# The last routed group taken apart: layernorm and logits in two pieces, one more shared expert at the end, a third set of weight buffers

## The chip, the cores and the metric

The kernel runs on one core of one Trainium2 chip. The metric is the device time of one launch in microseconds (us); of several runs the median is taken. In the profile's rows PE is TensorE's matmuls, PEld its weight loads, DVE VectorE, ACT ScalarE, POOL GpSimd, SP the engine that queues most DMAs.

## The reference, cut to what matters

There are 64 batches of 128 tokens with 128 features, each with 77 context rows of 96 features.

```python
x = x + xattn(layernorm(x), ctx_768)       # 16 heads of 64, softmax over 77 keys
x = x + ffn(layernorm(x))

def ffn(x2):                               # x2: 8192 tokens of 128
    logits = x2 @ router_w.T               # 8 experts
    _, idx = top_k(softmax(logits), 2)
    gate = scatter(logits at idx)
    for e in range(8):                     # inner width 176
        moe += gate[:, e] * ((silu(x2 @ w1[e].T) * (x2 @ w3[e].T)) @ w2[e].T)
    return moe + shared expert of the same shape, for all tokens
```

The first line is the attention with its residual, the second the mixture of experts: each token goes to two of eight experts and to a shared one.

## The kernel before

**Attention.** The 64 batches form 16 groups of four (`G = 4`, `T = 512` tokens). A unit is one batch and eight of its heads; there are 128 units, and each is worked on in two steps, so that group g occupies the steps 16g to 16g + 15 of a written plan (`at(step, ...)`). In one pass of the loop, TensorE computes the scores of the unit two ahead (`scores`, tile ps), the product with the values of a finished batch (`out`, tile py), and the transposed weights (tile pa). VectorE takes maxima and sums (tiles mx, sc, sm), ScalarE the exponentials, GpSimd the normalization (tile at).

**Routing.** When a group's batches are done, a `Router` takes it over: `stats` (layernorm statistics on VectorE, and one power on GpSimd, tile rs_f), `normed` (ScalarE scales the rows into the tile pay), `transpose` (TensorE, tile pxT_f, copied by ScalarE into x2T), `logits` (TensorE, tile pl), `choose` and `choose_second` (sixteen small VectorE operations that find two experts), `place` (the rank of each token among those of its expert; matmuls into pr, then VectorE up to the tile row), and `send`: eight indirect DMAs from GpSimd that scatter the rows to DRAM (tensor sent). The shared expert follows (`shared_up`, `shared_rest`, `shared_down`), and x1 is put away in DRAM (`park`).

**Experts.** The groups form three sets (`SETS = (9, 5, 2)`). After a set's last group, `tables` works out which 128-row block belongs to which expert. Four blocks make a `Quad`; the sets have 20, 12 and 6 of them. A quad loads its rows (xb, SP), copies its four experts' weights within SBUF (`weights`, tile w: two copies on ScalarE, two on VectorE), transposes (pt), multiplies (`first`: p; `rest`: ph; `down`: pq), and scatters its result (tile y) with four indirect DMAs from GpSimd (`answer`, tensor answers). A `Combine` per group loads x1 and the two answers of each token (tile ya), adds them on VectorE and stores them.

**Order.** All engines run what is written in the order in which the plan emits it; the order of each engine's instructions is fixed when the program is built. Quads of a set are spread evenly over the steps of the next set's groups. The last seven quads of the second set (`KEPT = 7`), the shared expert of the last group and the six quads of the last set run behind the attention, in `ending()`, as 14 jobs in a row; what is written in `ahead_of[k]` is emitted ahead of job k. There the last group, number 15, is routed: statistics ahead of job 0, transpose and logits ahead of 1, choice ahead of 2, ranks ahead of 3, sends ahead of 4, tables ahead of 5.

In the text "quad 1.7" is quad 7 of the second set (the sets are numbered 0, 1, 2). Only buffers that matter here: the tile y has two, pay one, w eight, vo (values) four, ya three.

Of the kernel before, what the change touches and what calls it, by code (L numbers as in the profile page):

```python
# [8 lines left out]
F32 = mybir.dt.float32  # L9
# [26 lines left out]

KEPT = 7

# [22 lines left out]
def xattn_moe_kernel(  # L61
# [32 lines left out]
    def weights_of(engine, w, q, n, name):  # L94

        to = ffn.tile([128, WALL], F32, tag="w", name=f"{name}_{q}", bufs=2 * QUAD)
        to = to[:, : 4 * n].rearrange("p (m d) -> p m d", d=n)
        engine.dma_start(out=to, in_=w[:, 4 * q : 4 * (q + 1), :])
        return to
# [161 lines left out]
    class Norm:  # L261
# [4 lines left out]

        def stats(self):
            st = small.tile([128, G, 6], F32, tag="st", name=f"st_{self.name}")
            self.mv = small.tile([128, G, 2], F32, tag="mv", name=f"mv_{self.name}")
            for b in range(G):  # L270
                nc.vector.bn_stats(st[:, b, :], self.src[:, b, :])
            for b in range(G):
                nc.vector.bn_aggr(self.mv[:, b, :], st[:, b, :])
            ve = small.tile([128, G], F32, tag="ve", name=f"ve_{self.name}")
            nc.vector.tensor_scalar(ve, self.mv[:, :, 1], EPS, None, ALU.add)
            self.rs = small.tile([128, G], F32, tag="rs", name=f"rs_{self.name}")
            nc.gpsimd.tensor_tensor(self.rs, ve, mhalf, ALU.pow)

        def scale(self, to):

            self.to = to
            shift = small.tile([128, G], F32, tag="shift", name=f"shift_{self.name}")
            nc.vector.scalar_tensor_tensor(shift, self.mv[:, :, 0], -1.0, self.rs, ALU.mult, ALU.mult)
            for b in range(G):
                nc.scalar.activation(
                    to[:, b, :],
                    self.src[:, b, :],
                    AF.Identity,
                    scale=self.rs[:, b : b + 1],
                    bias=shift[:, b : b + 1],  # L290
                )

        def transposed(self, tag):
            pt = bank(f"pxT_{self.name}")
            for b in range(G):
                nc.tensor.transpose(pt[:, b * 128 : (b + 1) * 128], self.to[:, b, :], ident)
            xT = grp.tile([D, T], F32, tag=tag, name=f"{tag}_{self.name}")
            nc.scalar.copy(xT, pt)
            return xT

# [4 lines left out]
    class Attention:  # L305
# [75 lines left out]
        def values(self, p, i):  # L381

            bs = (2 * p, 2 * p + 1)
            if i == 0:
                for b in bs:
                    self.vo[b] = bat.tile([128, NT, D], F32, tag="vo", name=f"vo_{self.g}_{b}", bufs=4)
                    k = KS * (self.g % 2 * G + b)
                    nc.sync.dma_start(
                        out=self.vo[b][:, 8:, :],
                        in_=last_values[self.g // 2][k : k + KS, :].rearrange("k (s t d) -> (k s) t d", t=2, d=D),  # L390
                    )
                if p == 0:
                    self.cM = first_keys.pop(self.g)
# [108 lines left out]
    class Router:  # L502
# [12 lines left out]

        def stats(self):
            self.norm.stats()

        def normed(self):

            self.pay = grp.tile([128, 2, G, DW], F32, tag="pay", name=f"pay_{self.g}", bufs=1)
            self.norm.scale(self.pay[:, 0, :, :D])

        def transpose(self):
            self.x2T = self.norm.transposed("x2T")
            nc.scalar.copy(self.pay[:, 1, :, :D], self.pay[:, 0, :, :D])

        def logits(self):
            pl = bank(f"pl_{self.g}")
            for b in range(G):  # L530
                nc.tensor.matmul(
                    pl[:, b * E : (b + 1) * E], self.x2T[:, b * NQ : (b + 1) * NQ], rw_sb, start=True, stop=True
                )
            self.lg = lg = self.t3("lg")
            nc.vector.tensor_copy(lg.rearrange("p b e -> p (b e)"), pl[:, : G * E])
            m = self.t2("gm")
            nc.vector.tensor_reduce(m, lg, AX.X, ALU.max)
            self.sc = sc = self.t3("gsc")
            nc.vector.tensor_tensor(sc, lg, wide(m, sc.shape), ALU.subtract)
            nc.scalar.activation(sc, sc, AF.Exp)  # L540
# [170 lines left out]
    class Quad:  # L711
# [19 lines left out]
        def weights(self, room=None):  # L731
# [3 lines left out]
            for k, (engine, copy) in enumerate(  # L735
# [3 lines left out]
                for j, e in enumerate(values(self.st.w_row[0:1, first : first + half], E - 1, engine)):  # L739
                    if room is None:  # L740
                        w = ffn.tile([128, WALL], F32, tag="w", name=f"w_{self.name}_{half * k + j}", bufs=2 * QUAD)
                    else:
                        w = room[:, (half * k + j) * WALL : (half * k + j + 1) * WALL]
# [47 lines left out]
    class Combine:  # L791


        def __init__(self, st, j, queue):
            self.st, self.j, self.queue = st, j, queue

        def load_x1(self):
            st, j = self.st, self.j
            self.ya = ffn.tile([128, 3, G, D], F32, tag="ya", name=f"ya_{st.i}_{j}", bufs=3)
            nc.sync.dma_start(out=self.ya[:, 0], in_=parked[st.start + j])  # L800

        def load_answers(self):
            st, j = self.st, self.j
            self.queue.dma_start(
                out=self.ya[:, 1:].rearrange("p c b d -> p (c b) d"),
                in_=answers[st.i][nb * 128 + j * 2 * T : nb * 128 + (j + 1) * 2 * T, :].rearrange(
                    "(p k) d -> p k d", p=128
                ),
            )

        def load(self):
            self.load_x1()
            self.load_answers()

        def add(self):
            for c in range(1, 3):
                nc.vector.tensor_tensor(self.ya[:, 0], self.ya[:, 0], self.ya[:, c], ALU.add)  # L817

        def store(self):
            g = self.st.start + self.j  # L820
            self.queue.dma_start(out=out[g * G : (g + 1) * G].rearrange("b t d -> t b d"), in_=self.ya[:, 0])

# [79 lines left out]
    for g in range(NG - 1):  # L902
        p = 16 * (g + 1)
        routing(g, p, (0, "stats"), (1, "normed"), (3, "transpose"), (4, "logits"), (5, "choose"), (6, "choose_second"))
    for st in sets:
        for g in range(st.start, min(st.start + st.n, NG - 1)):
            p = 16 * (g + 1)
            routing(g, p, (8, "place"), (11, "shared_up"), (12, "shared_rest"), (14, "shared_down"), (17, "park"))
            for k in range(4):
# [11 lines left out]
    for st, after in zip(sets, sets[1:]):  # L921
        quads = [Quad(st, q) for q in range(st.quads)]
        until = after.ready - 8 if after is not sets[-1] else end - 4
        if after is sets[-1]:
# [11 lines left out]
        if after is not sets[-1]:  # L936
            for j in range(st.n):
                c = Combine(st, j, nc.sync)
                at(p + 7 + 2 * j, c.load)
                at(p + 10 + 2 * j, c.add)  # L940
                at(p + 11 + 2 * j, c.store)

# [4 lines left out]
    def job_of(quad, n):  # L947
        job = {k: getattr(quad, k) for k in steps}
        if n % 4 > 1:
            job["weights"] = lambda: quad.weights(keys_room(f"w_{quad.name}"))  # L950
# [7 lines left out]
    def last(step, *args):  # L958
        return lambda: route(NG - 1, step, *args)

    blocks = [job_of(quad, n) for n, quad in enumerate(kept + [Quad(last_set, q) for q in range(last_set.quads)])]
    shared = {
        "first": last("shared_up", True),
        "rest": last("shared_rest", True),
        "down": last("shared_down"),
        "answer": last("park"),
    }
    jobs = blocks[:KEPT] + [shared] + blocks[KEPT:]

    ahead_of = {  # L970
        0: [last("stats"), last("normed")],
        1: [last("transpose"), last("logits")],
        2: [last("choose"), last("choose_second")],
        3: [last("place")],
        4: [last("send", c, b) for b in range(G) for c in range(2)],
        5: [lambda: tables(last_set)],
    }
    for k, job in enumerate(jobs):

        if k and "weights" in job:  # L980
            ahead_of.setdefault(max(k - 2, 6) if k > KEPT else max(k - 2, 0), []).append(job["weights"])

# [3 lines left out]
    for j in range(before_last.n):  # L986
        c = Combine(before_last, j, nc.sync)
        k = KEPT + 2 + j
        ahead(k, c.load)
        ahead(k + 1, c.add)  # L990
        ahead(k + 2, c.store)
    for j, queue in zip(range(last_set.n), (nc.sync, nc.scalar)):
        c = Combine(last_set, j, queue)
        ahead(len(jobs), c.load_x1)
        ahead(len(jobs) + 1, c.load_answers)
        ahead(len(jobs) + 2 + j, c.add)
        ahead(len(jobs) + 2 + j, c.store)

    def ending():
# [4 lines left out]
        for k in range(max(ahead_of) + 1):  # L1004
            do(k + 2, "load")
            for step in ahead_of.get(k, ()):
                step()
            do(k, "first")
            do(k + 1, "transpose")
            do(k, "rest")  # L1010
# [6 lines left out]
    at(end - 1, jobs[0]["transpose"])  # L1017
    at(end + 4, ending)

# [130 lines left out]
```

## Time and profile before

| | us |
|---|---|
| median of 13 runs | 992.62 |
| lowest and highest of them | 990.75 to 996.92 |
| the profiled execution, its own time | 990.87 |
| its span, first to last instruction | 989.2 |
| PE busy | 925.2 |
| POOL busy | 522.1 |
| DVE busy | 681.3 |

The span and the rows below it belong to the one profiled execution, which lies 1.75 us under the median. In the rows a line such as L781 is a line of the kernel before, "out<-in" names the tiles written and read, and a bracket gives the idle time of the engine before the instruction and what ended it.

### The profile page before, as it was taken

Reading aid. Unit: us, or ns where it says so; the run is one execution under the profiler, and the core shown is the slowest. Engines: PE = TensorE matmul, PEld = TensorE weight load, DVE = VectorE, ACT = ScalarE, POOL = GpSimd, SP = SyncE. Lnnn points to the kernel's source line nnn. Section 1 sums busy time; section 2 is a strip of 40 time slices with the busy share of each in tenths; the row PEclk is TensorE's granted clock in tenths of the full one; section 3 lists DMA queues with packets and bytes.
Section 4 is the critical chain, followed back from the end, with each engine's and each line's share of the span. In section 5 each row is a group of like instructions: output and inputs, shape, how many; then the busy total and the mean of one; then the engine's idle time right before and its main releaser. Section 6 shows DMA issues by size and latency. Waiting matters only on the chain. (4 is left out here: it accounts for less than half of the span.)

```text
span 989.2 us, 18933 instructions
## 1 busy us (share of the span) xinstructions
PE 925.2 (94%) x6136; PEld 770.7 (78%) x6136; DVE 681.3 (69%) x1768; ACT 652.5 (66%) x1420; POOL 522.1 (53%) x691
## 2 busy tenths in 40 slices
PE   7999999999999999999999999999999999869780
PEld 6787877787778878776888888887888787759580
DVE  4566776676767667778686776776676878957351
ACT  4776767676767667675776767666767676546550
POOL 3244563636364544636366375484474554726763
PEclk9999999999999999999999999999999999979796
DMA  5222212212222221122322222133131145643384
GB/s 171 76 61 70 68 43 78 76 49 71 74 68 66 76 73 61 48 84 78 92 77 66 81 84 72 42 90 94 47 99 32 52 124 176 177 140 94 96 255 146
DMA packets 81986, 87.21 MB, mean 88 GB/s; under 512 B 11488, under 2 KB 63456, under 8 KB 81888
## 3 DMA queue, kind: packets, MB, share of 16 engines
q1 hardware_dynamic: 66928, 57.34, 20.7%
q0 software_dynamic: 8960, 18.50, 5.7%
q10 hardware_dynamic: 6000, 10.16, 2.8%
q8 instruction: 49, 0.80, 0.3%
q14 instruction: 49, 0.40, 0.1%
HBM read 48.90 MB, written 37.06 MB: 87 GB/s over the span
## 5 line engine op out<-in xcount | busy, mean ns | idle before, releaser
L328 PEld LDWEIGHTS pk<-cT,wkq_sb 96*128 96x128 f32 x1024 | 157.9, 189 | 70.4 <-issue 42.8
L781 POOL DMA_INDIRECT answers<-y,to x152 | 150.9, 993 | 89.9 <-ACT y L777 38.3
L335 ACT COPY kx<-pk 128x308 f32<-128x308 f32 x256 | 104.4, 416 | 132.4 <-PE pk L328 126.1
L328 PE MATMUL pk<-cT,wkq_sb 96*128 96x154 f32 x1024 | 175.2, 294 | 1.1 <-DVE wkq_sb L246 0.8
L424 PEld LDWEIGHTS py<-vo,aT 128*128 128x128 f32 x1280 | 153.3, 191 | 11.6 <-ACT vo L402 1.1
L345 PE MATMUL ps<-kx,xgT 128*128 128x308 f32 x512 | 156.4, 426 | 5.3 <-DVE sc L356 4.7
L621 POOL DMA_INDIRECT sent<-pay,row x128 | 127.4, 995 | 60.7 <-DVE part L611 26.8
L424 PE MATMUL py<-vo,aT 128*128 128x128 f32 x1280 | 155.4, 276 | 0.8 <-ACT aT L417 0.7
L377 POOL TENSOR_TENSOR at<-sc,ri 128x512 f32<-128x512 f32 x64 | 67.2, 1050 | 168.3 <-DVE ri L369 113.6
L402 ACT COPY vo<-pv 64x512 f32<-64x512 f32 x256 | 147.1, 575 | 2.1 <-ACT vn L442 0.4
L397 PE MATMUL pv<-wvo_sb,cM 96*128 96x512 f32 x256 | 131.3, 595 | 1.4 <-DVE hr L499 0.8
L367 DVE TENSOR_REDUCE sm<-sc 128x8 f32<-128x616 f32 x128 | 101.2, 790 | 38.3 <-ACT sc L360 37.7
L360 ACT ACTIVATE sc<-sc,rs_a 128x616 f32<-128x616 f32 x128 | 104.9, 820 | 22.2 <-DVE sc L356 10.7
L375 POOL TENSOR_TENSOR at<-sc,ri 128x256 f32<-128x256 f32 x128 | 76.3, 619 | 81.0 <-DVE ri L369 27.1
L417 ACT COPY aT<-pa 128x512 f32<-128x512 f32 (+1 forms) x256 | 96.1, 429 | 31.3 <-PE pa L414 26.8
L345 PEld LDWEIGHTS ps<-kx,xgT 128*128 128x128 f32 x512 | 88.8, 189 | 32.8 <-DVE sc L356 5.8
L356 DVE TENSOR_TENSOR sc<-ps,mx 128x616 f32<-128x616 f32 x128 | 102.4, 800 | 12.9 <-DVE mx L354 0.5
L354 DVE TENSOR_REDUCE mx<-ps 128x8 f32<-128x616 f32 x128 | 98.4, 769 | 7.7 <-PE ps L345 6.4
L414 PE MATMUL pa<-ident,at 128*128 128x128 f32 x640 | 91.6, 274 | 0.0
L414 PEld LDWEIGHTS pa<-ident,at 128*128 128x128 f32 x640 | 75.3, 142 | 10.8 <-issue 10.7
L757 PE MATMUL p<-xT,w 128*128 128x128 f32 x608 | 77.2, 281 | 3.9 <-ACT xT L752 3.9
L757 PEld LDWEIGHTS p<-xT,w 128*128 128x128 f32 x608 | 73.4, 197 | 7.2 <-ACT xT L752 6.2
(146 smaller groups left out, 1422.9 us busy)
## 6 DMA issues: line engine op xcount, KB each, us to landing
xb<-sent SPq DMA_DIRECT2D x152, 65.0 KB
last_values<-vn ACTq DMA_DIRECT2D x32, 256.0 KB
vo<-last_values SPq DMA_DIRECT2D x64, 128.0 KB
ya<-answers SPq DMA_DIRECT2D x15, 512.0 KB
xg<-in_x_dram SPq DMA_DIRECT2D x16, 256.0 KB
xgT<-in_xT_dram SPq DMA_DIRECT2D x16, 256.0 KB
parked<-x SPq DMA_DIRECT2D x16, 256.0 KB
ya<-parked SPq DMA_DIRECT2D x16, 256.0 KB
```

Of the source, the lines that this page charges most:

```text
L328: nc.tensor.matmul(pk[:, k].rearrange("p (b k) -> p b k", k=NKV), wkq_sb[:, 2 * i + k, :], self.cT[:, 2 * p : 2 * (p + 1), :], start=True, ...
L335: nc.scalar.copy(self.kx[p][:, hs, :], pk)
L345: nc.tensor.matmul(ps[:, r, : 4 * NKV].rearrange("p (j k) -> p j k", k=NKV), self.xgT[:, ts], self.kx[p][:, h : h + 4, ks], start=True, st ...
L356: nc.vector.tensor_tensor(at, sc, over_keys(mx), ALU.subtract)
L360: nc.scalar.activation(at, at, AF.Exp, scale=self.norm.rs[:, b : b + 1])
L397: nc.tensor.matmul(pv, self.cM[:, p, KM * r : KM * (r + 2)], wvo_sb[:, h : h + 4, :], start=True, stop=True)
L402: nc.scalar.copy(self.vo[b][rows, 4 * t : 4 * (t + 1), :], pv[rows].rearrange("p (m d) -> p m d", d=D))
L414: nc.tensor.transpose(pa[:, j * NQ : (j + 1) * NQ], keys[:, c : c + 128], ident)
L424: nc.tensor.matmul(py[:, :D], aT[:, m, :], vo[:, m, :], start=(m == 0), stop=(m == NT - 1))
L621: ins = nc.gpsimd.indirect_dma_start(out=sent[st.i], out_offset=bass.IndirectOffsetOnAxis(ap=self.row[:, i : i + 1], axis=0), in_=self.pay ...
L757: nc.tensor.matmul(to[:m, ts], self.w[j][:, c : c + m], self.xT[:, ts], start=True, stop=True)
L781: ins = nc.gpsimd.indirect_dma_start(out=answers[st.i], out_offset=bass.IndirectOffsetOnAxis(ap=self.to[:, j : j + 1], axis=0), in_=self.y ...
```

## The change

It moves work and buffers; no arithmetic is added or dropped.

- The last set's second group is routed in two pieces. `stats`, `normed`, `transpose` and `logits` take a range of batches. Batches 0 to 2 of group 15 are normalized and get their logits inside the attention (steps end − 3 to end − 1), batch 3 follows ahead of and within job 0. Choice comes ahead of job 1, ranks and all sends ahead of job 2, tables ahead of job 4. The copy of pay for the second choice, formerly part of `transpose`, is a step of its own (`twice`), and the exponentials of the router are too (`exps`).
- `KEPT` is 5: two more quads of the second set run beside the attention (seven in the steps 240 to 252, formerly five). The shared expert of group 14 goes from there to the end, as a job of its own; the ending has 13 jobs: three quads, shared 14, two quads, shared 15, six quads of the last set.
- The first set's 20 quads end eight steps earlier (64 steps, formerly 72), and so do its combines; a combine's addition follows its load by two steps, formerly three.
- The weights have 12 buffers in place of 8, vo has three in place of four, ya two in place of three. The last set's groups keep x1 in SBUF and are not parked.

```diff
-KEPT = 7
+KEPT = 5
-        to = ffn.tile([128, WALL], F32, tag="w", name=f"{name}_{q}", bufs=2 * QUAD)
+        to = ffn.tile([128, WALL], F32, tag="w", name=f"{name}_{q}", bufs=3 * QUAD)
...
-        def stats(self):
+        def stats(self, bs=range(G)):
...
-            for b in range(G):
-                nc.vector.bn_stats(st[:, b, :], self.src[:, b, :])
+            for b in bs:
+                nc.vector.bn_stats(self.st[:, b, :], self.src[:, b, :])
...
-            nc.gpsimd.tensor_tensor(self.rs, ve, mhalf, ALU.pow)
+            nc.gpsimd.tensor_tensor(self.rs[:, of], self.ve[:, of], mhalf[:, of], ALU.pow)
...
-                    self.vo[b] = bat.tile([128, NT, D], F32, tag="vo", name=f"vo_{self.g}_{b}", bufs=4)
+                    self.vo[b] = bat.tile([128, NT, D], F32, tag="vo", name=f"vo_{self.g}_{b}", bufs=3)
...
+        def twice(self):
             nc.scalar.copy(self.pay[:, 1, :, :D], self.pay[:, 0, :, :D])
...
-            self.ya = ffn.tile([128, 3, G, D], F32, tag="ya", name=f"ya_{st.i}_{j}", bufs=3)
-            nc.sync.dma_start(out=self.ya[:, 0], in_=parked[st.start + j])
+            ya = ffn.tile([128, 3, G, D], F32, tag="ya", name=f"ya_{st.i}_{j}", bufs=2)
+            self.answers = ya[:, 1:]
+            if self.routers is None:
+                self.x1 = ya[:, 0]
+                self.queue.dma_start(out=self.x1, in_=parked[self.g])
+            else:
+                self.x1 = self.routers[self.g].x1
...
-            routing(g, p, (8, "place"), (11, "shared_up"), (12, "shared_rest"), (14, "shared_down"), (17, "park"))
+            routing(g, p, (8, "place"))
+            if g < NG - 2:
+                routing(g, p, (11, "shared_up"), (12, "shared_rest"), (14, "shared_down"), (17, "park"))
...
-        until = after.ready - 8 if after is not sets[-1] else end - 4
+        until = after.ready - 16 if after is not sets[-1] else end - 4
...
-                at(p + 10 + 2 * j, c.add)
-                at(p + 11 + 2 * j, c.store)
+                at(p + 9 + 2 * j, c.add)
+                at(p + 10 + 2 * j, c.store)
...
-        if n % 4 > 1:
+        if n % 5 > 2:
             job["weights"] = lambda: quad.weights(keys_room(f"w_{quad.name}"))
...
-    jobs = blocks[:KEPT] + [shared] + blocks[KEPT:]
-    ahead_of = {
-        0: [last("stats"), last("normed")],
-        1: [last("transpose"), last("logits")],
-        2: [last("choose"), last("choose_second")],
-        3: [last("place")],
-        4: [last("send", c, b) for b in range(G) for c in range(2)],
-        5: [lambda: tables(last_set)],
+    jobs = blocks[:3] + [shared(NG - 2)] + blocks[3:KEPT] + [shared(NG - 1)] + blocks[KEPT:]
+    most_of, rest_of = range(G - 1), range(G - 1, G)
+    at(end - 3, last("stats", most_of))
+    at(end - 2, last("normed", most_of))
+    at(end - 1, last("transpose", most_of), last("logits", most_of))
+    ahead_of = {
+        0: [last("stats", rest_of), last("normed", rest_of)],
+        1: [last("choose"), last("choose_second")],
+        2: [last("place"), last("twice")] + [last("send", c, b) for b in range(G) for c in range(2)],
+        4: [lambda: tables(last_set)],
     }
+    within = {0: [last("transpose", rest_of), last("logits", rest_of), last("exps")]}
...
-        c = Combine(before_last, j, nc.sync)
-        k = KEPT + 2 + j
+        c = Combine(before_last, j)
+        k = KEPT + 3 + j
...
-        c = Combine(last_set, j, queue)
-        ahead(len(jobs), c.load_x1)
-        ahead(len(jobs) + 1, c.load_answers)
+        c = Combine(last_set, j, queue, routers)
+        ahead(len(jobs) + 1, c.load)
...
             do(k, "first")
+            for step in within.get(k, ()):
+                step()
             do(k + 1, "transpose")
...
-    at(end + 4, ending)
+    at(end + 2, ending)
```

## The prediction

> **What bounds the kernel now.** I read the page first, for the busy shares and the slices.
>
> ```profile
> span 989.2 us, 18933 instructions
> PE 925.2 (94%) x6136; PEld 770.7 (78%) x6136; DVE 681.3 (69%) x1768; ACT 652.5 (66%) x1420; POOL 522.1 (53%) x691
> ...
> PE   7999999999999999999999999999999999869780
> ...
> POOL 3244563636364544636366375484474554726763
> PEclk9999999999999999999999999999999999979796
> ```
>
> TensorE is full from the second slice on and has holes only behind 840 us, where the clock falls too. GpSimd, at 53% of the span, is fullest there. So I asked for the end by windows; the columns are window, length, busy time (instructions) of PE, PEld, DVE, ACT, POOL, then granted clock, DMA share, GB/s.
>
> ```profile
> 800.00:840.00 40.00, 37.10 (x266) 31.59 (x265) 31.61 (x76) 28.34 (x63) 17.39 (x23) 1.00 0.57 172
> 840.00:876.00 36.00, 29.60 (x219) 26.73 (x217) 29.56 (x65) 16.70 (x37) 25.79 (x28) 0.95 0.68 196
> 876.00:893.60 17.60, 11.80 (x70) 10.91 (x71) 9.67 (x24) 11.02 (x24) 1.08 (x2) 0.62 0.17 44
> 893.60:920.90 27.30, 25.30 (x215) 23.30 (x213) 16.71 (x57) 17.29 (x38) 19.96 (x20) 0.99 0.34 97
> 920.90:977.20 56.30, 37.98 (x299) 35.02 (x298) 24.29 (x45) 27.01 (x64) 39.86 (x40) 0.86 0.61 183
> ```
>
> From 920.9 on GpSimd executes 40 indirect DMAs in 56.3 us while TensorE idles for 18. The timeline of POOL shows why (start, duration, line, what, idle before):
>
> ```profile
> 841.72 0.95 POOL L621 DMA_INDIRECT sent<-pay,row  x1 [0.62 <-DVE part L611]
> ...
> 876.10 1.04 POOL L277 TENSOR_TENSOR rs_f<-ve_f,mhalf 128x4 f32<-128x4 f32 x1
> 893.60 1.03 POOL L781 DMA_INDIRECT answers<-y,to  x1 [16.47 <-ACT y L777]
> ...
> 905.55 0.96 POOL L621 DMA_INDIRECT sent<-pay,row  x1 [0.30 <-issue]
> ...
> 919.65 0.96 POOL L621 DMA_INDIRECT sent<-pay,row  x1 [0.30 <-DMA sent<-pay,row]
> 920.91 0.96 POOL L781 DMA_INDIRECT answers<-y,to  x1 [0.30 <-DMA sent<-pay,row]
> ...
> 976.20 0.96 POOL L781 DMA_INDIRECT answers<-y,to  x1 [0.30 <-issue]
> ```
>
> An indirect DMA holds POOL for 0.96 us, and the next one starts 0.30 later: 1.26 each, 5.05 a quad. Group 14's sends start at 841.72, group 15's last one ends at 920.61. Behind that lie ten quads (50.5 us of POOL and 5.8 of gaps), then 12.0 us for the last load, addition and store. Ten quads follow the last send in the changed program's POOL order as well. So the end is the last send plus a tail, and the question is when that send comes. Two rows of DVE give the start of its chain:
>
> ```profile
> 840.07 0.18 DVE L592 TENSOR_TENSOR place<-pr,first_row 128x32 f32<-128x32 f32 x1
> ...
> 874.59 0.86 DVE L271 BATCH_NORM_STATS2 st_f<-x 128x6 f32<-128x128 f32 x4
> ```
>
> From group 15's statistics to its rank rows (901) pass 26 us. TensorE's holes lie on that chain:
>
> ```profile
> 877.91 1.63 PE L296 MATMUL pxT_f<-ident,pay 128*128 128x128 f32 x4 [4.66 <-ACT pay L285]
> ...
> 883.43 1.88 PE L531 MATMUL pl<-rw_sb,x2T_f 128*128 128x8 f32 x8 [3.88 <-ACT x2T_f L298]
> ...
> 924.56 0.45 PE L750 MATMUL pt<-ident,xb 128*128 128x128 f32 x1 [3.61 <-DMA xb<-sent]
> ```
>
> **The change, along that chain.** Its times come from the profiled execution: span 989.2, own time 990.87, 1.75 below the median of 992.62. I compare the last send before, 78.9 us after S = 841.72 (the start of group 14's sends), with the last send after.
>
> *Step 1, S moves back.* VectorE is full from 799.5 to 840 but for 6.6 us of waits (3.0 for ScalarE's a, 1.2 for rs, the rest below one each). In the changed order more stands ahead of group 14's place: five combine additions for three (2 x 1.41 = 2.8), two more weight copies (quads 1.3 and 1.4: 2 x 0.88 and 2 x 0.56 of issue = 2.9), u and h of quad 1.3 (1.5), ur and hr of quad 1.2 (1.4): 8.6. Did all waits fill up, 2 would remain; but they are waits on the tile's own chain, and ScalarE gets two more quads' copies in front of a (1.32 each), so up to 10 is possible. I take 7: S = 848.7. Group 14's shared expert, which leaves, stood behind place and gives nothing back here.
>
> *Step 2, S to the first power.* rs_f of batches 0 to 2 stands on POOL behind the 8 sends, 4 + 4 + 3 answers of quads 1.2 to 1.4 and two pairs of at products: 19 x 1.26 + 2 x 1.58 + 1.04 = 28.2, without idle time, since these quads' y come earlier. It ends at 876.9.
>
> *Step 3, to the second power.* TensorE now has transposes and logits of batches 0 to 2 ahead of the last attention product py (in the order before, py came first). From rs_f: scaling 1.3, two weight copies and the copies of aT and x2T on ScalarE 3.1, six logit matmuls at half clock 1.4, the transposes of quad 1.7 0.9, py 3.6 (2.2 at full clock, 4.4 at half), pq of quad 1.6 1.8, its y 0.4; its four answers 5.05 stand on POOL ahead of the second rs_f, 1.1. Sum 18.7 (16.1 at full clock): 895.6. The answers of quad 1.5 fit in between.
>
> *Step 4, to the last send.* Shift and scaling 0.6, four weight copies on ScalarE 2.6, a and x2T 0.9, logits and transposes at half clock 1.2, ph 1.7; ar, ur and hr 2.1; 16 operations of the choice at 0.22, 3.6; u, h, ur, hr of quad 1.8 and to of 1.7, 3.0 (VectorE has them ahead of place). That is 15.7; then the 4 answers of quad 1.7 (5.05), whose to waits there, and 8 sends (10.1): 30.9. The last send ends at 926.5, against 920.6: 5.9 later. POOL's 16.5 us of idle are not gone, they stand now in two pieces, 6 ahead of quad 1.6 and 15 ahead of 1.7.
>
> *Step 5, the tail.* With two ya buffers, a load waits until the store two before has landed; the row of a store says 2.97 from issue to landing (959.62). VectorE has this addition ahead of h and to of the next quads. Five combines; two loads are late by about 2.4, and POOL's gaps (1.0 at 961.97) give part of it: I take 1.7, bounds 0 and 6 (two stores in full).
>
> Sum: 7 − 1.1 (28.2 + 18.7 + 30.9 = 77.8 for 78.9) + 1.7 = 7.6.
>
> At zero I count: the two quads beside the attention in TensorE's time (2 x 4.88 − 4.35 for the shared expert = 5.4 there, the same less behind; TensorE waits for POOL in both); 12 buffers of w (they only let copies start earlier; quads two steps apart need them); three vo (a load waits for a py of the same pass, four passes ahead of its use; without that cover SP stands for 2.2); the earlier quads and combines of set 0 (TensorE is 96 to 100% busy there whatever the spacing; ±2 for a load that is not there two steps later); the missing x1 loads (at 963.38, long before the answers' load at 978.45); twice (0.63 on ScalarE behind y of quad 1.7, while POOL still waits for to); the tables and their eight marker DMAs (5.7 on SP from 908.47 before; now some 9 of TensorE's work behind place, so they land about with the last send, and without that cover each us late is one at the end).
>
> The profile shows a half clock after TensorE's holes: 8.5 us of holes are followed by 16 p matmuls in 3.6 us that take 1.8 elsewhere. I have two such places now, and steps 3 and 4 hold 2.6 and 1.4 for them. The Trainium skill ("TensorE: Matmul & The Clock Gate", Part 1) says that an idle window of about 3.4 us halves the clock and about 3.4 us of work restore it. By it each place would cost half of 3.4, together 3.4 in place of my 4.0; the sum would be 7.0. The rule speaks against a change that makes two holes out of one.
>
> **The rivals.**
>
> *Faster.* TensorE reaches py without having waited for rs_f: by work alone at 868.2 + 6.0 = 874.2 (two quads less the last pq, less shared, plus transposes and logits). Then the second power ends at 882.6 (pq 1.8, y 0.4, answers 5.05, power 1.1), the last send at 913.5, 7.1 earlier; with the tail's 1.7 that is −5.4. It needs step 2's end by about 867, so S by 839. Against it: place already came at 840.07, with less in front. A weaker form, S at its lower bound and the clock never halved, gives 2 − 1.1 − 4.0 + 1.7 = −1.4.
>
> *No difference.* VectorE's waits swallow nearly all of the extra (S + 2) and the ya ring costs nothing: +0.9. For it: DVE's 69%; against: the waits have causes of their own.
>
> *Slower still.* The at products of the last two units stand behind the sends on POOL and pa waits for them; I count some 4 us of cover. If S slips by the full 10, steps 3 and 4 find TensorE late, some 3 more each: 10.6 + 6 = +16.6.
>
> **How the numbers follow.** The forecast +7.6, on the median 1000.2, has 0.66, with a range of its own of 995 (S + 2) to 1006 (S + 10 and a tail 2.6 longer). Faster by the first rival 0.17, no difference 0.09, much slower 0.08. A difference of 0.2%, 2 us, is about what a measurement can tell. Faster by more than that: 0.17. Within: 0.09. Slower: 0.74. The range of 8 in 10 goes from 990 (it leaves out the strong form of the first rival) to 1010.
>
> **What would show it.** Right: group 14's first send some 7 us later against its first quad; rs_f (128x3) behind three answers, with a hole of 5 us or more on PE ahead of pxT_f; a second hole; the last send near 926; POOL idle 10 us or more ahead of quad 1.7's answers; nine quads and a tenth behind the last send as before. Wrong: S unmoved and py before 875; the last send before 918; a tail that isn't 68 to 71 us from the last send to the end, for then something other than POOL sets it.

## The result, and the profile after

The changed kernel takes 1009.59 us (median of 10 runs, 1008.04 to 1012.3) where the kernel before takes 992.69 beside it: ratio 1.0167, 95% interval 1.0153 to 1.0181. It is slower, by 16.9 us, as forecast in direction and inside the range, but more than twice the +7.6 of the forecast. The profiled execution itself took 1013.75 us (span 1012.0), 4.2 above the kernel's median; that of before lay 1.75 below its own.

The page of the changed kernel, the rows that answer to those of before:

```profile
span 1012.0 us, 18905 instructions
PE 938.5 (93%) x6136; PEld 782.8 (77%) x6136; DVE 684.5 (68%) x1773; ACT 653.2 (65%) x1421; POOL 522.5 (52%) x692
...
PE   7999999999999999999999999899999898849881
...
POOL 3344563636365363635365475475565524753753
PEclk9999999999999999999999999999999998968895
```

TensorE does the same 6136 multiplications and is busy 13 us longer, and it now has slices below 9 well ahead of the end. The stations of GpSimd (timeline of POOL: start, duration, line, what, idle before) follow:

```profile
861.79 0.96 POOL L635 DMA_INDIRECT sent<-pay,row  x1 [0.62 <-DVE part L625]
...
889.21 0.89 POOL L279 TENSOR_TENSOR rs_f<-ve_f,mhalf 128x3 f32<-128x3 f32 x1
903.15 0.96 POOL L795 DMA_INDIRECT answers<-y,to  x1 [6.65 <-ACT y L791]
907.92 0.58 POOL L279 TENSOR_TENSOR rs_f<-ve_f,mhalf 128x1 f32<-128x1 f32 x1
925.48 1.06 POOL L795 DMA_INDIRECT answers<-y,to  x1 [16.97 <-ACT w L758]
...
939.89 0.96 POOL L635 DMA_INDIRECT sent<-pay,row  x1 [0.31 <-issue]
```

The two pieces of idle time that were forecast as 6 and 15 are there, as 6.65 and 16.97. What is not as forecast is the first row: S, the first send of group 14, at 861.79 for a forecast of 848.7.

To compare single profiles I set the starts equal by the scores of unit 8 (51.74 before, 54.38 after: 2.64 of start-up; over the profiles below it varies from −0.26 to +2.86 beside before, whatever the kernel). "Tail" is from the end of the last send to the end of the last recorded operation.

| kernel | S, starts equal | S to end of last send | tail | ratio to before |
|---|---|---|---|---|
| before | 841.72 | 78.89 | 65.56 | 1 |
| changed | 859.15 | 79.06 | 67.48 | 1.0167 |

So of the growth 17.4 us lie ahead of S, 0.2 between S and the last send, 1.9 in the tail: 19.5. With 2.64 of start-up and 0.7 behind the last recorded operation that is the 22.8 between the two spans; by the medians, whose profiled executions stand off in opposite directions, it is 16.9. Another 1.7 of the 17.4 belongs to this one execution: behind a wait of TensorE of 1.65 us, ahead of the scores of unit 81, its clock was halved from 467.23 to 470.64. a_nosplit below, the same program up to S, has no such piece there, and with starts equal its S is 857.29. Start-up and this piece, 4.3 together, are about what the profiled execution stands above the median.

How the 17.4 came about is seen in two windows, unit 80 to S and, of it, unit 120 to S (busy time of PE, PEld, DVE, ACT, POOL with instructions in brackets; then granted clock, DMA share, GB/s). Before, after, and the changed kernel with one constant put back (a_spread72, below):

```profile
455.00:841.72 386.72, 373.67 (x2601) 318.81 (x2599) 286.77 (x714) 267.64 (x591) 219.00 (x268) 1.00 0.28 82
786.16:841.72 55.56, 52.62 (x366) 44.41 (x364) 46.21 (x113) 37.89 (x83) 29.93 (x39) 1.00 0.50 149
```

```profile
457.67:861.79 404.12, 383.66 (x2649) 328.91 (x2648) 297.75 (x732) 272.26 (x601) 220.65 (x269) 0.98 0.31 91
794.44:861.79 67.35, 59.73 (x398) 51.42 (x397) 54.05 (x126) 40.57 (x89) 26.08 (x34) 0.92 0.56 170
```

```profile
454.92:848.03 393.11, 380.06 (x2661) 325.51 (x2659) 292.49 (x723) 271.54 (x601) 220.31 (x270) 1.00 0.29 85
786.04:848.03 61.99, 59.01 (x426) 51.10 (x424) 52.01 (x122) 41.75 (x93) 30.92 (x40) 1.00 0.55 160
```

TensorE's idle time in the long window is 13.05 us before (386.72 − 373.67), 20.46 after, and again 13.05 in the third. The changed kernel thus pays 6.39 us of TensorE work for the quads that moved up (380.06 − 373.67), 7.4 of additional idle time, and 3.6 of multiplications at a lower clock (383.66 − 380.06, at 0.98), in which the 1.7 at 467 are contained: 17.4.

### The profile page after: what moved, and what is told of

It reads as the page before. It is cut to its first block, busy times and chain, and to the rows that moved or that the text cites. A ratio compares the mean times of both kernels' runs of the same rounds, so it can differ in the third digit from the quotient of the medians.

```text
span 1012.0 us, 18905 instructions
## 1 busy us (share of the span) xinstructions
PE 938.5 (93%) x6136; PEld 782.8 (77%) x6136; DVE 684.5 (68%) x1773; ACT 653.2 (65%) x1421; POOL 522.5 (52%) x692
## 5 line engine op out<-in xcount | busy, mean ns | idle before, releaser
L334 PEld LDWEIGHTS pk<-cT,wkq_sb 96*128 96x128 f32 x1024 | 160.9, 193 | 70.4 <-issue 44.6
L334 PE MATMUL pk<-cT,wkq_sb 96*128 96x154 f32 x1024 | 178.3, 298 | 0.6 <-DVE wkq_sb L246 0.6
L351 PE MATMUL ps<-kx,xgT 128*128 128x308 f32 x512 | 159.8, 433 | 9.5 <-DVE sc L362 9.0
L430 PEld LDWEIGHTS py<-vo,aT 128*128 128x128 f32 x1280 | 156.5, 195 | 12.8 <-ACT vo L408 2.8
L430 PE MATMUL py<-vo,aT 128*128 128x128 f32 x1280 | 158.6, 279 | 1.6 <-ACT vo L408 1.4
```

Source lines behind the costliest of these rows:

```text
L334: nc.tensor.matmul(pk[:, k].rearrange("p (b k) -> p b k", k=NKV), wkq_sb[:, 2 * i + k, :], self.cT[:, 2 * p : 2 * (p + 1), :], start=True, ...
L351: nc.tensor.matmul(ps[:, r, : 4 * NKV].rearrange("p (j k) -> p j k", k=NKV), self.xgT[:, ts], self.kx[p][:, h : h + 4, ks], start=True, st ...
L430: nc.tensor.matmul(py[:, :D], aT[:, m, :], vo[:, m, :], start=(m == 0), stop=(m == NT - 1))
```

## The experiments

The runs fall into four groups, each on one chip and beside the kernel before, whose medians there were 993.01 (a_spread72, a_x1own, a_nosplit, b_kept5), 993.66 (a_lateadd, a_s72_x1own, a_s72_kept7, b_late), 1036.80 (a_s72_nosplit, b_adds, b_sh14, b_late3) and 992.71 us (the rest). In the third group everything is 4% longer, so only its ratios are used.

**1. The constant that I counted at nothing (a_spread72).**

```diff
-        until = after.ready - 16 if after is not sets[-1] else end - 4
+        until = after.ready - 8 if after is not sets[-1] else end - 4
```

> The changed kernel, with the quads of set 0 spread over 72 steps again instead of 64 (their combine additions then come 8 steps later too). Theory A (what I counted at zero, the denser quads of set 0, cost TensorE about 5.6 us between units 80 and 121): the offset of the attention units against the kernel before falls from 8.3 us at unit 120 to about 3, the first send of group 14 comes 3 to 6 us earlier than 861.8, and the time is 1004 to 1007 us. Rival B (the offset at unit 120 is only work of the quads done earlier, and is paid back before the first send): the first send stays within 1.5 us, time 1008 to 1011 us. Rival C (the additions that come 8 steps later now stand in front of group 14's choice): first send later, time over 1011 us.

Measured: 999.45 us, ratio 1.0079 (1.0060 to 1.0099). Over half of the loss is gone, more than any theory gave. With starts equal S is 848.08, S to last send 78.51, tail 67.20. This is the kernel that my forecast described: 999.45 for 1000.2, S 848.1 for 848.7.

**2. Spacing or additions? (a_lateadd)** The constant moves the 20 quads and, with the last of them, nine combines. Here the quads stay at 64 steps and only the combines go back.

```diff
-                at(p + 7 + 2 * j, c.load)
-                at(p + 9 + 2 * j, c.add)
-                at(p + 10 + 2 * j, c.store)
+                at(p + 15 + 2 * j, c.load)
+                at(p + 17 + 2 * j, c.add)
+                at(p + 18 + 2 * j, c.store)
```

> The changed kernel, set 0's quads over 64 steps as in it, but the loads, additions and stores of its nine combines 8 steps later, where the 72-step spacing has them. Of the 11.0 us by which group 14's first send comes later than with 72 steps (starts set equal), 5.6 were lost before unit 120 (no addition stands there in either kernel) and 5.4 behind it. Theory A (the quads' spacing costs the 5.6 on TensorE, the early additions the 5.4 behind unit 120): offset at unit 120 as in the changed kernel (+5.6 against the kernel before), first send 4 to 5.5 us earlier than the changed kernel's, time 1003.5 to 1006 us. Rival B (all 11 come of the spacing, since units 121 to 127 then stand with no quad beside them): 1008 to 1011 us. Rival C (all of it comes of the additions): 999 to 1001 us.

Measured: 1003.89 us, ratio 1.0104 (1.0085 to 1.0124), in time as theory A. The stations tell more. At unit 120 it is 4.0 behind the kernel before, starts equal, for the changed kernel's 5.6. Contrary to the expectation one addition (788.97) does stand ahead of that unit, but the difference is the halved clock at 467: a_nosplit, with that addition and without that piece, is 3.8 behind there. From unit 120 to S this kernel takes 60.25 us, the changed kernel 67.35 (its row is above) and a_nosplit 67.33:

```profile
791.43:851.68 60.25, 57.65 (x407) 50.27 (x406) 49.41 (x119) 40.12 (x88) 25.71 (x35) 0.97 0.53 158
```

So the early combines cost 7.1 us at S (0.63% of the time), 5.0 of it in TensorE's idle time (67.35 − 59.73 = 7.6 for 60.25 − 57.65 = 2.6). At S this kernel is only 2.3 behind a_spread72: quads done early are partly paid back. In the time that is 0.25%, and the intervals of the two ratios overlap. VectorE's timeline in the changed kernel shows the early combines, eight additions ahead of the place of group 14 at 860.14; in the kernel before, a_lateadd and a_spread72 three or four stand there:

```profile
788.97 1.42 DVE L830 TENSOR_TENSOR ya<-ya 128x512 f32<-128x512 f32 x2
...
807.29 1.42 DVE L830 TENSOR_TENSOR ya<-ya 128x512 f32<-128x512 f32 x2 [2.57 <-DMA ya<-answers]
...
853.13 1.42 DVE L830 TENSOR_TENSOR ya<-ya 128x512 f32<-128x512 f32 x2
860.14 0.18 DVE L606 TENSOR_TENSOR place<-pr,first_row 128x32 f32<-128x32 f32 x1
```

**3. The ring of ya (a_x1own, a_s72_x1own).** The third addition waits for its answers. SP's queue (SPq) shows why they came late; sent<-nobody are marker DMAs of a table, out_dram<-ya is a combine's store:

```profile
794.07 5.21 SPq L691 DMA_DIRECT2D sent<-nobody  x8
799.38 0.41 SPq L834 DMA_DIRECT2D out_dram<-ya  x1
802.44 0.33 SPq L818 DMA_DIRECT2D ya<-parked  x1
```

The store stands behind the eight marker DMAs of set 1's `tables`, which the earlier combines now meet; the next load waits on the landing of that store, because ya has two buffers; the load of the answers is queued behind it (802.83). A windows table of 3.4 us pieces shows what followed on TensorE:

```profile
808.00:811.40 3.40, 0.70 (x5) 0.45 (x3) 3.21 (x6) 0.00 (x0) 1.37 (x2) 1.00 0.62 185
811.40:814.80 3.40, 3.26 (x11) 2.70 (x12) 2.63 (x5) 3.34 (x6) 0.00 (x0) 0.58 0.70 217
```

TensorE is busy for 0.70 us of one piece, then granted 0.58 in the next. In a_x1own the x1 rows have three buffers of their own (u has one, and two start-up tiles move, to make room):

```diff
-            ya = ffn.tile([128, 3, G, D], F32, tag="ya", ..., bufs=2)
-            self.answers = ya[:, 1:]
+            self.answers = ffn.tile([128, 2, G, D], F32, tag="ya", ..., bufs=2)
...
-                self.x1 = ya[:, 0]
+                self.x1 = ffn.tile([128, G, D], F32, tag="yx", ..., bufs=3)
```

> The changed kernel, with the x1 rows of a combine in a ring of their own with three buffers; the answers keep two. A load of x1 then no longer waits for the store two before. Theory A (the ring of two costs about 3 us between units 121 and 122 and about 2 in the tail): VectorE's addition behind unit 121 waits under 0.5 us instead of 2.57, the first send of group 14 comes about 3 us earlier, the tail from last send to end shrinks by 1 to 2.6 us, time 1004 to 1006.5 us. Rival B (the answers' buffers, or the VectorE work itself, set that wait): no change, 1008.5 to 1010.5 us. Rival C (the tail alone gains): 1007 to 1008.5 us.

Measured: 1005.74 us, ratio 1.0136 (1.0114 to 1.0158), as A: S 3.5 earlier, 2.9 of it behind unit 120 (64.41 for 67.35), tail 65.85 for 67.48, and the granted clock from unit 120 to S is 1.00 for 0.92 (0.95 in a_nosplit). The addition still waits 1.25 us, not under 0.5, so the ring was not its only cause.

> The changed kernel with set 0's quads over 72 steps and x1 of the combines in a ring of its own with three buffers: both repairs together. Alone they gave 999.45 and 1005.74 us. Theory A (the ring's cost in the tail, 1.6 us, stays and goes; its cost at units 121 to 127 is already gone with the 72 steps): 997 to 998.5 us, tail from last send to end as in the kernel before. Rival B (the two gains of 10.1 and 3.9 us add up): 995 to 996 us. Rival C (no gain, the tail is set by GpSimd's answers): 999 to 1000.5 us.

Measured: 1000.12 us, ratio 1.0072 (1.0049 to 1.0094), rival C. With 72 steps the ring costs nothing that shows: 1.0072 for 1.0079. The tail is 66.63 for 67.20; the ring as the cause of the tail, my step 5, is not shown.

**4. The split.** Three kernels undo it or leave it alone. a_nosplit:

```diff
-    most_of, rest_of = range(G - 1), range(G - 1, G)
-    at(end - 3, last("stats", most_of))
-    at(end - 2, last("normed", most_of))
-    at(end - 1, last("transpose", most_of), last("logits", most_of))
+    rest_of = range(G)
```

> The changed kernel with the split undone: statistics, shift and scaling of all four batches of group 15 ahead of job 0, its transposes and logits within job 0 behind the last attention product. Everything else, the two shared experts and the moved quads among it, as changed. Theory A (the last attention product py is held up by the transposes and logits of batches 0 to 2, which wait for the power that stands behind GpSimd's 19 indirect DMAs): the power comes once, at about the first send + 39, the last send some 5 to 8 us earlier, time 1002 to 1005 us. Rival B (the split is neutral, since GpSimd's sends and answers must be issued in either case): 1008 to 1011 us. Rival C (the split does gain, by taking three batches' logits off the chain): 1012 to 1018 us.

Measured: 1006.34 us, ratio 1.0141 (1.0121 to 1.0161). A by the stations, S to last send 74.90 us for 79.06; the time lies between A and B.

The same on 72 steps, a_s72_nosplit and, on another chip, a_s72_nosplit_r:

> The changed kernel with 72 steps for set 0's quads and the split undone, both. Alone they gave 999.45 and 1006.34 us for 1009.59. Theory A (the split costs GpSimd idle time in two pieces wherever the first send lies; undone, the last send comes 4 us sooner behind the first, 74.9 us for 79.1): first send at 848, last send's end at 923, time 995 to 997 us. Rival B (with 72 steps the split costs nothing): 998.5 to 1000.5 us. Rival C (the split costs as much as in the kernel with KEPT 7, 11 us): 988 to 991 us.

> The changed kernel with 72 steps for set 0's quads and the split undone (the kernel of a_s72_nosplit) once more, on a chip whose TensorE does not stand still for nothing the profile shows. Theory A (undoing the split brings the last send 4 us closer to the first): first send at 848, last send's end near 923, 995 to 997.5 us. Rival B (with 72 steps the split costs nothing): 998.5 to 1000.5 us.

Measured: ratios 1.0033 (1.0013 to 1.0053) and 1.0036 (1.0024 to 1.0048), 996.38 us in the latter, where the kernel with the split has 1.0079 (999.45 us): theory A, 3 us by the times and 4 by the ratios. GpSimd's timeline there has one power and one piece of idle time:

```profile
887.45 1.05 POOL L279 TENSOR_TENSOR rs_f<-ve_f,mhalf 128x4 f32<-128x4 f32 x1
907.95 1.06 POOL L795 DMA_INDIRECT answers<-y,to  x1 [19.46 <-issue]
...
922.35 0.95 POOL L635 DMA_INDIRECT sent<-pay,row  x1 [0.30 <-issue]
```

19.46 us idle, where a_spread72 has 6.02 + 16.95 = 22.97. The 3.5 more are what the last send loses (78.5 to 75.0).

b_kept5 is the other way round: the kernel before, with `KEPT = 5`, shared 14 at the end and the buffers of the changed kernel, but undivided layernorm and old set 0.

```diff
-KEPT = 7
+KEPT = 5
-        3: [last("place")],
-        4: [last("send", c, b) for b in range(G) for c in range(2)],
-        5: [lambda: tables(last_set)],
+        3: [last("place")] + [last("send", c, b) for b in range(G) for c in range(2)],
+        4: [lambda: tables(last_set)],
...
+    jobs = blocks[:3] + [shared(NG - 2)] + blocks[3:KEPT] + [shared(NG - 1)] + blocks[KEPT:]
```

> The kernel before with the move of the work alone: two more quads of set 1 beside the attention, group 14's shared expert at the end, twelve weight buffers, three of vo, two of ya, the choice's order of the changed kernel; group 15's layernorm and logits undivided, set 0's quads and combines as before. Theory A (the changed kernel's loss is the sum of set 0's spacing 5.6, the ring of ya 3 to 5, and VectorE's work ahead of place 8.5, less a power that comes in one piece): time 998 to 1003 us, the first send of group 14 at 849 to 854 us. Rival B (the work move costs it all): 1007 to 1012 us. Rival C (the work move gains, and the split loses): 985 to 992 us.

Measured: 996.22 us, ratio 1.0039 (1.0024 to 1.0054), a little under A's range: from the other end it comes to the same as a_s72_nosplit. The work move costs 0.4%.

And the split without the work move, a_s72_kept7:

```diff
-KEPT = 5
+KEPT = 7
-    jobs = blocks[:3] + [shared(NG - 2)] + blocks[3:KEPT] + [shared(NG - 1)] + blocks[KEPT:]
+    jobs = blocks[:KEPT] + [shared(NG - 1)] + blocks[KEPT:]
```

> The split of group 15's layernorm and logits alone: set 0 over 72 steps, two quads and group 14's shared expert back beside the attention as in the kernel before (the twelve weight buffers and the two of ya stay). Theory A (the work move costs step 1's 6 to 7 us, and the split nothing): first send of group 14 at 842 to 844 us, last send 78 to 79 us behind it, time 994 to 996.5 us. Rival B (the split by itself gains, since TensorE reaches the last attention product sooner): the last send 72 to 75 us behind the first one, 986 to 991 us. Rival C (the split by itself costs: the power behind more answers, the ring of two): 998 to 1002 us.

Measured: 1005.03 us, ratio 1.0124 (1.0101 to 1.0148): no theory had it that high. S is 843.00, hardly moved, and the last send ends 77.49 behind it. The sends stand two jobs earlier in GpSimd's order, but come only 1.4 us sooner behind the first one; GpSimd idles instead (30.9 us between first and last send, 22.0 in the kernel before), and twelve quads are left behind them for ten (tail 77.43).

```profile
881.55 0.96 POOL L795 DMA_INDIRECT answers<-y,to  x1 [11.93 <-ACT y L791]
...
905.59 1.05 POOL L795 DMA_INDIRECT answers<-y,to  x1 [18.39 <-ACT a L481]
```

Putting a step earlier in an order moves it only if what it waits for comes earlier too.

**5. Which engine sets S? (b_adds)** The kernel before, with its combines of set 0 taken away from in front of place: five with additions at steps 249 to 257, four beside the first jobs of the end.

```diff
-            for j in range(st.n):
+            for j in range(5):
...
-                at(p + 10 + 2 * j, c.add)
+                at(p + 17 + 2 * j, c.add)
...
+    for j in range(5, sets[0].n):
+        c = Combine(sets[0], j, nc.sync)
+        ahead(j - 1, c.load)
+        ahead(j, c.add)
+        ahead(j, c.store)
```

> The kernel before with set 0's nine combines later: five with additions at steps 249 to 257 for 242 to 250, four beside the first jobs of the end. No addition of theirs is left in front of group 14's place (three were, 1.42 us each). Theory A (TensorE's work sets the first send, its idle time between units 80 and 127 is 13.05 us in the kernel before and in the changed one with 72 steps alike, and three additions fit into VectorE's waits): first send within 1 us of 841.7, time 991.5 to 994 us. Rival B (VectorE sets it: each addition ahead of place costs its 1.42 us): first send 3 to 4 us earlier, time 988.5 to 990.5 us. Rival C (four more additions behind group 15's choice cost more there): 995 to 998 us.

Measured: ratio 1.0037 (1.0013 to 1.0060), so the time is rival C's. On S, A holds: 55.38 us from unit 120 to S, where a kernel on the same chip that keeps its additions in front (b_sh14) has 55.39. The S of the kernel before is not VectorE's.

**6. The shared expert alone (b_sh14, b_sh14_r).** The kernel before with only this part of the change:

```diff
-    jobs = blocks[:KEPT] + [shared] + blocks[KEPT:]
+    jobs = blocks[:5] + [shared(NG - 2)] + blocks[5:KEPT] + [shared(NG - 1)] + blocks[KEPT:]
```

> The kernel before with group 14's shared expert alone moved to the end, behind the sixth job (its row is parked there, as group 15's is). Theory A (TensorE is the bound between the first send and the first power, 4.35 us of it go behind the last send, where TensorE waits for GpSimd): last send 3 to 4 us earlier, tail as before, time 988.5 to 990.5 us. Rival B (the path to the last send goes over VectorE and the chain of the last attention product, so the 4.35 us only widen the holes): 991.5 to 994 us. Rival C (the tail grows by the parking and the load behind it): 994 to 997 us.

> The kernel before with group 14's shared expert alone moved to the end (the kernel of b_sh14) once more; on the slow chip its ratio was 0.9972. Theory A (TensorE is the bound between the first send and the power): power 3 to 4 us earlier than 876.1, last send 917 to 918 instead of 920.6, ratio 0.996 to 0.998. Rival B (the gain was that chip's: its TensorE stood still ahead of that shared expert): ratio 0.999 to 1.002.

Measured: ratios 0.9972 (0.9948 to 0.9996) and 0.9955 (0.9938 to 0.9971), 988.47 us for 992.71: theory A, and faster than both kernels.

```profile
872.54 1.04 POOL L277 TENSOR_TENSOR rs_f<-ve_f,mhalf 128x4 f32<-128x4 f32 x1
...
915.83 0.95 POOL L621 DMA_INDIRECT sent<-pay,row  x1 [0.30 <-DMA sent<-pay,row]
```

S is unmoved (841.74), the power comes 3.5 us sooner than in the kernel before (876.10), starts equal, the last send ends 3.8 sooner. The tail grows by 1.9, with all three buffers of ya; GpSimd's gaps there add up to 7.9 us for 5.4.

**7. Filling the hole (b_late, b_late3, b_late3_sh14).** b_late is the kernel before with transposes and logits of group 15 ahead of job 2 and choice, place a job later:

```diff
-        1: [last("transpose"), last("logits")],
-        2: [last("choose"), last("choose_second")],
-        3: [last("place")],
-        4: [last("send", c, b) for b in range(G) for c in range(2)],
+        2: [last("transpose"), last("logits")],
+        3: [last("choose"), last("choose_second")],
+        4: [last("place")] + [last("send", c, b) for b in range(G) for c in range(2)],
```

> The kernel before with the transposes and logits of group 15 one job later (ahead of job 2), choice, place and sends one job later too. Theory A (TensorE's 8.5 us of holes ahead of pxT_f and pl and the half clock behind them are filled with quad 1.4's matmuls; GpSimd issues one more quad's answers ahead of group 15's sends, in its 16.5 us of idle time): last send within 3 us of 920.6, nine quads behind it for ten, time 986 to 991 us. Rival B (the last send is what counts and comes later by a job's work, and the tail behind it does not shrink): 996 to 1001 us. Rival C (also fewer idle us of GpSimd in the tail): 975 to 985 us.

Measured: 993.27 us, ratio 0.9999 (0.9984 to 1.0014), no theory's. The sends kept their place in GpSimd's order, ten quads ahead of the end, and TensorE's hole only took another name. First a row of PE, then one of ACT:

```profile
882.33 3.78 PE L757 MATMUL p<-xT,w 128*128 128x128 f32 x16 [9.28 <-ACT xT L752]
```

```profile
877.23 1.65 ACT L285 ACTIVATE pay<-x,shift_f,rs_f 128x128 f32<-128x128 f32 x4 [6.10 <-DVE shift_f L283]
```

ScalarE held the copy of the next quad's xT behind a scaling that waited for the power. b_late3 puts that right and moves the sends too:

```diff
-        0: [last("stats"), last("normed")],
-        1: [last("transpose"), last("logits")],
...
+        0: [last("stats")],
+        1: [last("normed")],
+        2: [last("transpose"), last("logits")],
+        3: [last("choose"), last("choose_second")],
+        4: [last("place")],
+        5: [last("send", c, b) for b in range(G) for c in range(2)] + [lambda: tables(last_set)],
```

> The kernel before with all of group 15's chain behind the statistics one job later: shift and scaling ahead of job 1, transposes and logits ahead of 2, choice 3, place 4, sends and tables 5. In b_late ScalarE's scaling still stood ahead of its copy of the next quad's xT and TensorE waited 9.3 us for that copy; here the copy comes first. Theory A (the hole of 8 to 9 us ahead of the last group's transposes closes, GpSimd idles 8 us less between the first power and the last send; the last send comes 4 to 6 us later with nine quads behind it for ten): time 984 to 989 us. Rival B (the chain from the power to place is what counts, and it gets a job longer): 994 to 1000 us. Rival C (GpSimd's holes only move behind the last send, the tables coming late): 990.5 to 993.5 us.

> The kernel before with group 14's shared expert at the end and group 15's chain one job later (scaling ahead of job 1, transposes and logits 2, choice 3, place 4, sends and tables 5). Theory A (both shorten GpSimd's idle time ahead of the last send, 3 us and some 4): ratio 0.991 to 0.995. Rival B (the later chain only moves GpSimd's idle time behind the send, as on the slow chip): as b_sh14_r, within 0.002. Rival C (tables one job closer to the sends make the first quads of group 14 and 15 late): ratio 1.000 to 1.004.

Measured: ratio 0.9999 (0.9973 to 1.0025) alone, and 0.9951 (0.9932 to 0.9971) with shared 14 at the end, 988.87 us: rivals C and B, nothing clear of noise beyond b_sh14_r. GpSimd's longest wait ahead of the sends falls from 16.3 us (b_sh14_r) to 11.5 (b_late3_sh14), but the tail gets a wait of 5.03. Its gaps add up to 7.8 us as in b_sh14_r (7.9), with one quad fewer in it; why the medians are level all the same stays open.

**8. One quad (b_sh14_k6):** b_sh14 with `KEPT = 6`.

> b_sh14 with one more quad of set 1 beside the attention (six kept back for seven). Theory A (each moved quad delays the first send by 3.2 us, half of the 6.4 of two, and takes 5.05 us of answers from behind the last send): ratio 0.994 to 0.998. Rival B (the last power comes by a whole quad of TensorE later, 4.9, and the half clock behind it eats the rest): ratio 0.998 to 1.003.

Measured: ratio 1.0019 (1.0000 to 1.0038), 995.78 us: rival B. The power comes at 881.37 for 872.54, 8.7 later with starts equal, for one quad of 4.88 of TensorE; the tail, a quad shorter, gives back 2.3 of its 5.05 (65.1 for 67.5).

## Why the prediction was wrong

The parts, by the ratios along the chain of kernels from before to changed: work move 0.36% (a_s72_nosplit_r), split 0.43% (a_spread72 against it), denser quads 0.25% (a_lateadd), early combines 0.63%: 1.67%, each known to 0.2 or 0.3%. They hold for this order: without the work move the split cost far more (a_s72_kept7, 1.24%). The work move has two sides, the shared expert's gain of 0.45% (b_sh14_r) and the cost of the two quads with the new buffers, which no run separates.

- **The failed term stands in the list "at zero": "the earlier quads and combines of set 0 ... ±2".** It measures 11.1 us at S in the profile, 9.4 without the halved clock at 467, and some 9 us in the time (1.0167 against 1.0079). I argued from TensorE being "96 to 100% busy there whatever the spacing" and never followed where the combines went: eight additions stand ahead of place, where step 1 has "five combine additions for three", because I counted only from 799.5 on. At S, 2.3 are the quads' spacing and 7.1 the early combines. Of the latter 2.9 went with the ring of x1; the remaining 4.2 is about the length of the three additions more that stand between unit 120 and place (3 × 1.42 = 4.3, seven for a_lateadd's four). That these make it is argued; no run separates it further.
- **Step 1, S + 7, had the right size by the wrong engine.** With 72 steps S moves by 6.4. I had charged VectorE's 8.6 us of instructions less its waits, and put TensorE's two quads at zero. The windows show the reverse: TensorE's work +6.39, its idle time unchanged to the hundredth; and b_adds takes three additions away without moving S. That VectorE begins to set S at the additions of the changed kernel is likely, but not shown. The agreement of the size was luck.
- **Steps 2, 3 and 4 hold.** From S to the end of the first power 28.3 us (28.2 forecast), to the second 18.4 (18.7), to the last send's end 32.35 (30.9); together 79.06 for 77.8. But reading 79 for 79 as "neutral" hid that the split costs: undone, it is 74.9 to 75.0. Two opposite moves cancelled, since shared 14 leaving this stretch gains 3.8 there (b_sh14_r).
- **Step 5, 1.7:** 1.9 measured, but that the ring makes it is not shown. GpSimd's gaps account for it (1.17 + 2.57 + 3.56 = 7.3 for 0.78 + 3.63 + 1.01 = 5.4), and b_sh14_r has the same tail with three buffers. What makes the gaps stays open: with x1's own ring they are 5.8 and 6.1.
- **The rivals.** "Faster" needed S by 839 and TensorE at py by work alone; neither came. "Slower still", +16.6, has nearly the measured time by another path: S slipped by 17 rather than 10, and steps 3 and 4 did not grow by 3 each.
- **The clock.** The half clock was weighed only for the two holes behind S, where sizes held. It mattered ahead of S as well: from unit 120 to S the granted clock is 0.92 in the changed kernel and 1.00 with x1's own ring. The row at 808.00 has TensorE busy for 0.70 us of 3.40, and the clock fell. The Trainium skill ("TensorE: Matmul & The Clock Gate", Part 1) asks for an idle window of about 3.4 us; here the window need not be empty, and the measurement decides. The last section has a further case.

## What to carry to other kernels

When a change also shifts a cadence that looks idle-proof, list every instruction that the shifted loop emits, loads and stores included, and look what it newly meets on each queue; here the earlier combines met a table's markers on SP, two buffers, and the rank step on VectorE. Charge extra work ahead of a station first to the engine that is full there, and use the idle time of that engine, not the number of moved instructions, to tell which engine that is. A part that looks neutral inside a bundle deserves a run by itself: the gain here comes with a single part, the shared expert behind the last send, and no kernel is clearly better than the one that takes it alone (0.9955; 0.9951 for b_late3_sh14).

## What the runs showed of the hardware

- The half clock did not need an empty stretch, and the same stretch does not always halve it. In the changed kernel the granted clock changes at 467.23, 470.64, 811.97, 815.39, 839.28 and 846.11, whole multiples of 3.413 us apart. Ahead of the scores of unit 81 TensorE waits 1.65 us for VectorE (tile sc). In the changed kernel the last 3.41 us before the change at 467.23 (463.81 to 467.23) have TensorE busy 1.77 us, and 0.50 followed. In a_s72_x1own the same wait lies in a step from 461.60 to 465.01 (120 steps ahead of that profile's next change, at 874.62). TensorE is busy 1.76 us there, and 1.00 followed. Five of the 18 profiles have a halved piece there, and it costs 1.5 to 1.7 us. The busy share alone does not tell which it will be.
- On the chip of the third group of runs every kernel took some 4% longer. Its TensorE stood still for 1 to 5.7 us at a time with nothing that the profile shows as its cause, often ahead of the shared expert's multiplications (5.01 us at 809.93 in b_sh14) or between those of one quad. What holds it there stays open.
